# Ids for four blocks in one load, and the last block's single-field chunks moved behind 20 others

## The chip, the cores and the metric

The kernel runs on one core of a Trainium2 chip. The time is device microseconds from the first to the last instruction of one execution; the figure for a kernel is the median of several executions. A core has TensorE (PE in the profile: matrix multiplies and transposes, its weight loads shown as PEld), VectorE (DVE), ScalarE (ACT), GpSimd (POOL), SyncE (SP) and 16 DMA engines. Each of the engines runs its own list of instructions in order and waits for the others through semaphores.

## The reference

A recommender model scores 16384 users. Each user has 69 categorical fields (`batch_user`) and one item (`batch_label`), all of them row numbers of an embedding table of 100001 rows by 96 float32.

```python
u = emb[batch_user]                      # 16384 x 69 x 96
ql = emb[batch_label[:, 0]]              # 16384 x 96
q = broadcast(ql[:, None, :], u.shape)
z = concatenate([q, u, q - u, q * u], axis=-1)
h = dice(z @ W1 + b1, a1)                # 64 wide; dice is a gated activation with a sigmoid
att = (h @ W2 + b2) @ W3 + b3            # one number per user and field
pre = where(batch_user < ITEM_NUM, u * att, 0)
pooled = einsum('gf,bfe->bge', window, pre)      # fields summed into 10 groups
x = concatenate([pooled.reshape(B, G * E), ql], axis=-1)
h = dice(bn(x @ Wf1 + bf1), af1)         # 200 wide
h = dice(bn(h @ Wf2 + bf2), af2)         # 80 wide
return h @ Wf3 + bf3
```

So 16384 x 69 rows of 384 bytes have to be gathered, and each goes through a small network that gives its weight in the sum.

## The kernel before

The users are worked off in 32 blocks of 512. A block's rows come in 69 chunks of 512 rows. The first 64 chunks hold 8 users by 64 fields each; the last five hold one field each (fields 64 to 68) for all 512 users: these are the single-field chunks, "tails" in the code. Two chunks make a pair, and the program is laid out in steps, one pair entering per step: 32 x 69 / 2 = 1104 pairs.

```python
BLK = 512; NBLK = 32; FM = 64; NTAIL = 5; NMAIN = 64; NCH = 69      # NS = 8 users per main chunk
NCOL = NCH * 4 + 4                       # id columns of a block: 4 per chunk, 4 for the items
POOL_LAG = 8; CLOSE = 8
ipool = tile_pool(name="ipool", bufs=2)  # ids
upool = tile_pool(name="upool", bufs=14) # gathered rows of a pair
xpool = tile_pool(name="xpool", bufs=1)  # pre, x1, g1, x2
...
def load_ids(n):                                                    # L136
    t = ipool.tile([P, NCOL], I32, tag="ids", name=f"ids{n}")
    nc.sync.dma_start(out=t, in_=idx[n])                            # L138
    return t
ids = {0: load_ids(0)}
...
def chunk(c):                                                       # L256
    n, k = divmod(c, NCH)
    if n == NBLK - 1:
        k = (k - NTAIL) % NCH            # the last block begins with its tails
    return n, k
```

The main steps of a pair. A gather is one indirect DMA of 128 rows that GpSimd issues, eight per pair. TensorE turns the rows to put the 96 features on partitions; VectorE multiplies by the item's row; four matmul groups give the hidden layer; ScalarE and VectorE do the activation.

```python
def fetch(i, between=None):
    u = upool.tile([P, 8, E], F32, tag="u", name=f"u{i}")
    ...
            for t in range(4):
                gather(rows, u[:, 4 * j + t, :], ids[n][:, 4 * k + t : 4 * k + t + 1])          # issued at L249
                nc.tensor.transpose(ptr[:, t * P : (t + 1) * P], u[:, 4 * j + t, :], ident)     # L305
    ...  # quT = ptr * item row (VectorE, L308 or L315 for a tail), uT = copy of ptr (ScalarE, L317)
def hidden(i, uT, quT):
    ...  # ph = A.uT + Wp.quT (L330, L334; for a tail L327, L332, L334), y = dice(ph) (L336 to L338)
def attend_rows(b, n): ...               # attention numbers of n pairs, L345
def spread(b, n): ...                    # turned, times the group window, L362 and L367
def pool(i):                             # 8 steps after fetch, main chunks only
    ...  # acc = u.T @ rw, 16 small matmuls (L389); VectorE copies the sums to pooled (L398)
def attend_tail(i, j, y, uT):            # tails only, 3 steps after fetch
    ...  # pres[n][:, k - NMAIN, :] = (attention + bb) * uT (L354, L355)
```

A row buffer `u` is free for the next pair when its transposes and its pooling are done; a tail isn't pooled, so its buffer is free after the transposes. When a block's chunks are through, its top network runs in ten steps. The first steps of each half read `pres` (five times), then the item row and the ten `pooled` groups (L428).

```python
        pres[n] = xpool.tile([E, NTAIL, BLK], F32, tag=f"pre{n == NBLK - 1}", name=f"pre{n}")   # L511
...
for n in range(NBLK):                                               # L547
    first, end = n * NCH // 2, ((n + 1) * NCH - 1) // 2
    if n > 0:
        at(first - 20, lambda n=n: ids.__setitem__(n, load_ids(n)))
        at(first - 14, ...head_gather...)                           # item rows, 4 gathers
        at(first - 11, ...head_turn...); at(first - 9, ...head_rows...)
    if n < NBLK - 1:
        for s, work in enumerate(top_steps(n, slice(0, BLK))):
            at(end + POOL_LAG + 4 + s, work)
```

The last block's top network is done in four quarters while its last pairs still run.

Of the kernel before, what the change touches and what calls it, by code (L numbers as in the profile page):

```python
# [32 lines left out]
F32 = mybir.dt.float32  # L33
I32 = mybir.dt.int32
# [4 lines left out]
P = 128  # L39
B, F, E, G = 16384, 69, 96, 10  # L40
# [5 lines left out]
BLK = 512  # L46
NBLK = B // BLK
FM = 64
NTAIL = F - FM
NS = BLK // FM  # L50
NMAIN = BLK // NS
NCH = NMAIN + NTAIL
NQ = BLK // P
NT = NCH * 4
NCOL = NT + NQ
# [4 lines left out]

POOL_LAG = 8

CLOSE = 8


# [45 lines left out]
def rec_kernel(  # L111
    ctx: ExitStack,
    tc: tile.TileContext,
    idx: bass.AP,
    emb: bass.AP,
    rows: bass.AP,
# [4 lines left out]
    nc = tc.nc  # L121

    const = ctx.enter_context(tc.tile_pool(name="const", bufs=1))
    ipool = ctx.enter_context(tc.tile_pool(name="ipool", bufs=2))
# [5 lines left out]
    xpool = ctx.enter_context(tc.tile_pool(name="xpool", bufs=1))  # L130

    def by_field(ap):

        return ap.rearrange("e (s o) -> e s o", o=1).to_broadcast([ap.shape[0], NS, FM])

    def load_ids(n):  # L136
        t = ipool.tile([P, NCOL], I32, tag="ids", name=f"ids{n}")
        nc.sync.dma_start(out=t, in_=idx[n])  # L138
        return t

    ids = {0: load_ids(0)}


    wn = const.tile([P, NEAR.width], F32, name="wn")
# [31 lines left out]
    for i in range(2):  # L176
        t = const.tile([E + 1, BLK], F32, name=f"qT{i}")
# [78 lines left out]
    def chunk(c):  # L256

        n, k = divmod(c, NCH)
        if n == NBLK - 1:
            k = (k - NTAIL) % NCH  # L260
        return n, k

    def head_gather(n):

        q = bpool.tile([P, NQ, E], F32, tag="q", name=f"q{n}")
        for k in range(NQ):
            gather(emb, q[:, k, :], ids[n][:, NT + k : NT + k + 1])
        return q

    def head_turn(n, q):  # L270
        pq = ps_x.tile([E, BLK], F32, tag="x", name=f"pq{n}")
        for k in range(NQ):
            nc.tensor.transpose(pq[:, k * P : (k + 1) * P], q[:, k, :], ident)
        nc.vector.tensor_copy(qTs[n % 2][0:E, 0:BLK], pq)

    def head_rows(n):

        for h in range(2):
            pc = ps_x.tile([P, NMAIN // 8, H1], F32, tag="x", name=f"pc{n}_{h}")
            for k in range(NMAIN // 8):  # L280
                x = (h * NMAIN // 8 + k) * 4 * NS
                nc.tensor.matmul(pc[E:P, k, :], qTs[n % 2][:, x : x + 4 * NS], Cq, start=True, stop=True)  # L282
            nc.scalar.copy(As[n % 2][E:P, h * NMAIN // 8 : (h + 1) * NMAIN // 8, :], pc[E:P])
# [9 lines left out]
    def fetch(i, between=None):  # L293

        u = upool.tile([P, 8, E], F32, tag="u", name=f"u{i}")
        uT = []
        quT = tpool.tile([E, 2, 512], F32, tag="quT", name=f"quT{i}")
        for j in range(2):
            if j == 1 and between:
                between()  # L300
            n, k = chunk(2 * i + j)
            ptr = ps_tr.tile([E, 512], F32, tag="tr", name=f"ptr{i}_{j}")
            for t in range(4):
                gather(rows, u[:, 4 * j + t, :], ids[n][:, 4 * k + t : 4 * k + t + 1])
                nc.tensor.transpose(ptr[:, t * P : (t + 1) * P], u[:, 4 * j + t, :], ident)  # L305
            q = qTs[n % 2][0:E]
            if k < NMAIN:
                nc.vector.tensor_tensor(  # L308
                    quT[:, j, :].rearrange("e (s f) -> e s f", f=FM),
                    ptr.rearrange("e (s f) -> e s f", f=FM),  # L310
                    by_field(q[:, k * NS : (k + 1) * NS]),
                    ALU.mult,
                )
            else:
                nc.vector.tensor_tensor(quT[:, j, :], ptr, q[:, 0:BLK], ALU.mult)  # L315
            uT.append(room(k))
            nc.scalar.copy(uT[j][0:E], ptr)  # L317
        return u, uT, quT
# [98 lines left out]
    def top1(n, cols, h, part, p1):  # L417

        if part == 0:
            p1 = ps_m.tile([DH, BLK], F32, tag="m", name=f"p1_{n}_{h}_{cols.start}")[:, cols]  # L420
        for k in range(part * KTOP // 4, (part + 1) * KTOP // 4):
            if k < NTAIL:
                w, x = V[:, k], pres[n][:, k, cols]
            elif k == NTAIL:
                w, x = wf1[:, G], qTs[n % 2][0:E, cols]
            else:
                w, x = wf1[:, k - NTAIL - 1], pooled[n][:, k - NTAIL - 1, cols]
            nc.tensor.matmul(p1, w[:, h * DH : (h + 1) * DH], x, start=(k == 0), stop=(k == KTOP - 1))  # L428
        if part < 3:
            return p1  # L430
        g1 = xpool.tile([DH, BLK], F32, tag="g1", name=f"g1_{n}_{h}_{cols.start}")[:, cols]
        dice(x1s[n][:, h, cols], g1, p1, bf1c[h], dice1[h])

    def top2(n, cols):
        x2 = xpool.tile([D2, BLK], F32, tag="x2", name=f"x2_{n}_{cols.start}")[:, cols]
        g2 = xpool.tile([DH, BLK], F32, tag="g1", name=f"g2_{n}_{cols.start}")[0:D2, cols]
        p2 = ps_m.tile([D2, BLK], F32, tag="m", name=f"p2_{n}_{cols.start}")[:, cols]
        for i in range(2):
            nc.tensor.matmul(p2, wf2[:, i, :], x1s[n][:, i, cols], start=(i == 0), stop=(i == 1))
        dice(x2, g2, p2, bf2c, dice2)  # L440
        return x2

    def top3(n, cols, x2):
        k0, k1 = cols.start // P, cols.stop // P
        p3 = ps_m.tile([P, k1 - k0], F32, tag="m", name=f"p3_{n}_{cols.start}")
        for k in range(k1 - k0):
            nc.tensor.matmul(p3[:, k : k + 1], x2[:, k * P : (k + 1) * P], wf3, start=True, stop=True)
        nc.vector.tensor_scalar(res[:, n * NQ + k0 : n * NQ + k1], p3, bf3c, None, ALU.add)
# [9 lines left out]
    def top3_last(x2):  # L458

        p3 = ps_m.tile([1, P], F32, tag="m", name="p3_last")  # L460
        nc.tensor.matmul(p3, wf3, x2, start=True, stop=True)
        r = ypool.tile([P, 512], F32, tag="y", name="r1")[0:1, 0:P]
        nc.vector.tensor_scalar(r, p3, bf3c[0:1], None, ALU.add)
        nc.sync.dma_start(out=out[B - P :].rearrange("p o -> o p"), in_=r)

    pooled, pres, x1s, x2s, qs, us, hs, ys, bands, rws, p1s = ({} for _ in range(11))

    def top_steps(n, cols):


        def half(h, part):
            if n not in x1s:
                x1s[n] = xpool.tile([DH, 2, BLK], F32, tag="x1", name=f"x1_{n}")
            p1s[n] = top1(n, cols, h, part, p1s.get(n))

        steps = [lambda h=h, part=part: half(h, part) for h in range(2) for part in range(4)]
        steps.append(lambda: x2s.__setitem__(n, top2(n, cols)))
        if n * BLK + cols.stop < B:
            steps.append(lambda: top3(n, cols, x2s.pop(n)))
        else:  # L480
            steps.append(lambda: top3_last(x2s.pop(n)))
        return steps
# [22 lines left out]
    def fetch_of(k, between=()):  # L505
        def work():
            for j in range(2):
                n = chunk(2 * k + j)[0]
                if n not in pooled:
                    pooled[n] = bpool.tile([E, G, BLK], F32, tag="pooled", name=f"pooled{n}")  # L510
                    pres[n] = xpool.tile([E, NTAIL, BLK], F32, tag=f"pre{n == NBLK - 1}", name=f"pre{n}")  # L511
            u, uT, quT = fetch(k, lambda: [w() for w in between])
            us[k], hs[k] = u, (uT, quT)

        return work
# [4 lines left out]
    def at(step, *work):  # L520
        plan.setdefault(step, []).extend(work)

    close = NPAIR - CLOSE
    for i in range(close):
# [22 lines left out]
    for n in range(NBLK):  # L547
        first, end = n * NCH // 2, ((n + 1) * NCH - 1) // 2
        if n > 0:
            at(first - 20, lambda n=n: ids.__setitem__(n, load_ids(n)))  # L550
            at(first - 14, lambda n=n: qs.__setitem__(n, head_gather(n)))
            at(first - 11, lambda n=n: head_turn(n, qs.pop(n)))
            at(first - 9, lambda n=n: head_rows(n))
        if n < NBLK - 1:
            for s, work in enumerate(top_steps(n, slice(0, BLK))):
                at(end + POOL_LAG + 4 + s, work)
    for f in range(NTAIL):
        at(2 + 2 * f, lambda f=f: tail_weights(f))

# [77 lines left out]
```

## Time and profile before

Three executions took 13199.77 to 13208.66 us, median 13202.15 us. One was recorded by the profiler: a span of 13196.5 us.

| engine | busy us | share of the span | instructions |
|---|---|---|---|
| PE (matmul) | 8794.3 | 67% | 41797 |
| PEld (weight load) | 4570.3 | 35% | 41797 |
| DVE | 3032.1 | 23% | 5324 |
| ACT | 3167.2 | 24% | 4969 |
| POOL | 8455.0 | 64% | 8966 |

The gathers move 440.98 MB over the span, and the DMA engines are busy for some 17% of it. The ids come in 32 loads of 140 KB.

How such a profile is read: a group of instructions is named by its line, engine and operation, with `out<-in`; the busy time of a group stands beside the idle time of the engine before it and what ended that idle time (the releaser). "issue" is idle time without a wait that the profile shows, and "remote" or "another core or an unknown queue" is a release whose source the records don't hold. The chain of waits follows the last instruction back to what let each step start. Starts and ends of matmuls are partly modelled: an instruction that TensorE has taken in need not have finished when its bar ends.

### The profile page before, as it was taken

The numbers are of one execution on the slowest core, as the hardware profiler recorded it, in microseconds if no ns is written. First come the engines' busy times: TensorE is split into PE (matmuls) and PEld (weight loads), VectorE is DVE, ScalarE is ACT, GpSimd is POOL, SyncE is SP. The second block draws the span as 40 slices with busy tenths as digits, with TensorE's granted clock in tenths as the row PEclk, the third lists the DMA queues.
The fourth block names the chain that finished last, engine by engine and source line by source line (L and its number), as shares of the span: only waits on it lengthen the run. The fifth ranks groups of instructions, "written<-read, shape, count | busy, mean of one in ns | idle before, by whom it ended". The sixth has DMA issues, their size and how long they took to land.

```text
span 13196.5 us, 108603 instructions
## 1 busy us (share of the span) xinstructions
PE 8794.3 (67%) x41797; PEld 4570.3 (35%) x41797; DVE 3032.1 (23%) x5324; ACT 3167.2 (24%) x4969; POOL 8455.0 (64%) x8966
## 2 busy tenths in 40 slices
PE   4666666667666676666766667676677666677657
PEld 2333333333333333333333333333333333333334
DVE  2222222222222222222222222222222222222222
ACT  1222222222222222222222222222222222222222
POOL 6666666666666666666666666666666666666664
PEclk6677777777777777777777677777777777777777
DMA  1111111111111111111111111111111111111111
GB/s 38 35 35 34 34 35 34 35 36 34 33 35 34 35 35 34 35 35 35 35 34 35 34 35 34 34 35 35 35 35 35 34 34 34 35 34 35 35 33 22
DMA packets 292259, 454.06 MB, mean 34 GB/s; under 512 B 143906, under 2 KB 148258, under 8 KB 291618
## 3 DMA queue, kind: packets, MB, share of 16 engines
q0 software_dynamic: 286720, 440.98, 16.8%
q8 instruction: 335, 5.49, 0.2%
q1 hardware_dynamic: 4882, 4.90, 0.1%
q14 instruction: 178, 1.46, 0.0%
q10 hardware_dynamic: 144, 1.24, 0.0%
HBM read 446.47 MB, written 0.07 MB: 34 GB/s over the span
## 4 chain that ended last, share of the span: by engine, by line
PE 55%; issue 19%; another core or an unknown queue 16%; POOL 3%; ACT 3%; DVE 3%; DMA 1%; DVEq 0%; POOLq 0%
PE acc L389 11%; PE ptr L305 10%; PE ph L330 9%; PE ph L334 9%; PE p L428 7%; PE prow L345 4%; POOL u L249 3%; PE patt L362 1%; DVE quT L308 1%; PE pa L354 1%; ACT uT L317 1%; ACT y L337 1%; PE ph L327 1%; PE pc L282 1%
## 5 line engine op out<-in xcount | busy, mean ns | idle before, releaser
L249 POOL DMA_INDIRECT u<-in_rows,ids x8832 | 8333.3, 944 | 4574.9 <-issue 2366.2
L389 PE MATMUL acc<-rw,u 128*96 128x20 f32 x16384 | 1934.7, 260 | 1825.7 <-issue 1468.4
L389 PEld LDWEIGHTS acc<-rw,u 128*96 128x96 f32 x16384 | 1921.8, 198 | 2070.5 <-issue 1650.4
L305 PE MATMUL ptr<-ident,u 128*96 128x128 f32 x8832 | 1607.8, 318 | 1428.3 <-issue 1111.7
L305 PEld LDWEIGHTS ptr<-ident,u 128*96 128x96 f32 x8832 | 1087.4, 144 | 2773.9 <-issue 2183.1
L317 ACT COPY uT<-ptr 96x512 f32<-96x512 f32 x2208 | 1283.3, 581 | 3085.5 <-DVE quT L308 1941.0
L336 ACT ACTIVATE y<-ph 128x512 f32<-128x512 f32 x1104 | 659.5, 597 | 5154.5 <-remote 2718.6
L334 PE MATMUL ph<-quT,wn 96*64 96x512 f32 x4416 | 1692.6, 745 | 178.2 <-issue 168.5
L338 DVE TENSOR_TENSOR y<-ph,y 128x512 f32<-128x512 f32 x1104 | 763.5, 692 | 4382.3 <-ACT y L337 2352.5
L330 PE MATMUL ph<-uT,A 128*64 128x512 f32 x4096 | 1633.2, 800 | 140.7 <-issue 136.2
L308 DVE TENSOR_TENSOR quT<-ptr,qT 96x512 f32<-96x512 f32 x2048 | 1336.9, 680 | 1405.4 <-remote 961.0
L398 DVE COPY pooled<-acc 96x160 f32<-96x160 f32 x1009 | 429.9, 426 | 3473.4 <-remote 2069.0
L337 ACT ACTIVATE y<-y,wn,na1c 128x512 f32<-128x512 f32 x1104 | 897.6, 813 | 36.7
L334 PEld LDWEIGHTS ph<-quT,wn 96*64 96x64 f32 x4416 | 446.6, 172 | 1225.4 <-issue 1223.3
L345 PE MATMUL prow<-y,v 128*32 128x512 f32 x2208 | 634.2, 792 | 246.1 <-issue 143.8
L428 PE MATMUL p<-pooled,wf 96*100 96x512 f32 (+1 forms) x1400 | 622.3, 587 | 1.5 <-issue 1.3
L330 PEld LDWEIGHTS ph<-uT,A 128*64 128x64 f32 x4096 | 280.7, 161 | 678.3 <-issue 659.4
L347 ACT COPY row<-prow 128x512 f32<-128x512 f32 (+1 forms) x277 | 161.9, 584 | 1428.4 <-remote 899.3
L362 PE MATMUL patt<-ident,row 128*128 128x128 f32 x1108 | 247.5, 343 | 253.5 <-issue 167.4
L428 PE MATMUL p<-pre,V 96*100 96x512 f32 (+1 forms) x700 | 370.7, 663 | 31.0 <-issue 23.2
L428 PEld LDWEIGHTS p<-pooled,wf 96*100 96x100 f32 x1400 | 236.6, 181 | 297.0 <-issue 296.7
L367 DVE SCALAR_TENSOR_TENSOR rw<-patt,bb,wn 128x320 f32<-128x320 f32 x554 | 273.6, 534 | 146.2 <-remote 84.2
(66 smaller groups left out, 2125.1 us busy)
## 6 DMA issues: line engine op xcount, KB each, us to landing
u<-in_rows,ids POOLq DMA_INDIRECT x8832
ids<-in_idx SPq DMA_DIRECT2D x32, 140.0 KB
q<-in_emb,ids POOLq DMA_INDIRECT x128
wf<-in_far ACTq DMA_DIRECT2D x1, 1209.0 KB
wn<-in_near SPq DMA_DIRECT2D x1, 236.0 KB
out<-r SPq DMA_DIRECT2D x1, 63.5 KB
out<-r SPq DMA_DIRECT2D x1, 0.5 KB
```

The lines of the kernel that those rows point to most:

```text
L249: nc.gpsimd.indirect_dma_start(out=dst, out_offset=None, in_=table, in_offset=bass.IndirectOffsetOnAxis(ap=index, axis=0),)
L305: nc.tensor.transpose(ptr[:, t * P : (t + 1) * P], u[:, 4 * j + t, :], ident)
L308: nc.vector.tensor_tensor(quT[:, j, :].rearrange("e (s f) -> e s f", f=FM), ptr.rearrange("e (s f) -> e s f", f=FM), by_field(q[:, k * NS ...
L317: nc.scalar.copy(uT[j][0:E], ptr)
L330: nc.tensor.matmul(p, As[n % 2][:, k // 4, :], uT[j], start=True, stop=False)
L334: nc.tensor.matmul(p, Wp, quT[:, j, :], start=False, stop=True)
L336: nc.scalar.activation(y, ph, AF.Sigmoid, scale=S_DICE)
L337: nc.scalar.activation(y, y, AF.Identity, bias=a1c, scale=na1c)
L338: nc.vector.tensor_mul(y, ph, y)
L345: nc.tensor.matmul(pr[32 * k : 32 * (k + 1), :], v2, ys[b + k], start=True, stop=True)
L389: nc.tensor.matmul(pa[:, j, 2 * t : 2 * t + 2, :].rearrange("e n g -> e (n g)"), u[:, 4 * j + t, :], rw[:, t, j, :], start=True, stop=True,)
L428: nc.tensor.matmul(p1, w[:, h * DH : (h + 1) * DH], x, start=(k == 0), stop=(k == KTOP - 1))
```

## The change

Three things change. The ids of block 0 are loaded alone, and then those of four blocks at a time, so that 32 loads become 9. In the last block, the single-field chunks no longer come first; 20 main chunks (`EARLY`) come before them. And the last block's `pre` rows no longer have a buffer of their own: all blocks use one, for which block 30's top network is begun earlier and done two steps at a time. The last two save room in SBUF, which the larger id tiles need.

```diff
+NIDS = 4
+EARLY = 20
...
+    ids = {0: const.tile([P, NCOL], I32, name="ids0")}
+    nc.sync.dma_start(out=ids[0], in_=idx0)
+
     def load_ids(n):
-        t = ipool.tile([P, NCOL], I32, tag="ids", name=f"ids{n}")
-        nc.sync.dma_start(out=t, in_=idx[n])
-        return t
-
-    ids = {0: load_ids(0)}
+        t = ipool.tile([P, NIDS, NCOL], I32, tag="ids", name=f"ids{n}")
+        nc.sync.dma_start(out=t.rearrange("p b n -> p (b n)"), in_=idx[(n - 1) // NIDS])
+        for k in range(NIDS):
+            ids[n + k] = t[:, k, :]
...
         n, k = divmod(c, NCH)
-        if n == NBLK - 1:
-            k = (k - NTAIL) % NCH
+        if n == NBLK - 1 and k >= EARLY:
+            k = NMAIN + k - EARLY if k < EARLY + NTAIL else k - NTAIL
         return n, k
...
-                    pres[n] = xpool.tile([E, NTAIL, BLK], F32, tag=f"pre{n == NBLK - 1}", name=f"pre{n}")
+                    pres[n] = xpool.tile([E, NTAIL, BLK], F32, tag="pre", name=f"pre{n}")
...
-            at(first - 20, lambda n=n: ids.__setitem__(n, load_ids(n)))
+            if n % NIDS == 1:
+                at(first - 20, lambda n=n: load_ids(n))
...
-        if n < NBLK - 1:
+        if n < NBLK - 2:
             for s, work in enumerate(top_steps(n, slice(0, BLK))):
                 at(end + POOL_LAG + 4 + s, work)
+        elif n == NBLK - 2:
+            for s, work in enumerate(top_steps(n, slice(0, BLK))):
+                at(end + POOL_LAG + s // 2, work)
...
+    groups = np.concatenate([ids[1:], ids[:1]], axis=0).reshape(-1, NIDS, P, NCOL)
...
-        "idx": ids,
+        "idx0": ids[0],
+        "idx": groups.transpose(0, 2, 1, 3).reshape(-1, P, NIDS * NCOL),
```

(Cut: the new argument `idx0` of the kernel function, and blank lines. The last group of four is blocks 29, 30, 31 and, to fill it up, block 0 again.)

More of the change, by code (lines that the diff above doesn't have):

```diff
@@ L113, in rec_kernel @@
     tc: tile.TileContext,
+    idx0: bass.AP,
     idx: bass.AP,
```

## Prediction

> **What bounds the kernel now.** I read the page first (engines, clock, chain), then the list of waits, then the waits on the id loads, then the place where the change acts, the last block.
>
> The page, parts 1, 2, 4 and 5 (a group's columns: busy us, mean ns of one, idle us before it and its main releaser):
>
> ```profile
> span 13196.5 us, 108603 instructions
> PE 8794.3 (67%) x41797; PEld 4570.3 (35%) x41797; DVE 3032.1 (23%) x5324; ACT 3167.2 (24%) x4969; POOL 8455.0 (64%) x8966
> PEclk6677777777777777777777677777777777777777
> ...
> PE 55%; issue 19%; another core or an unknown queue 16%; POOL 3%; ACT 3%; DVE 3%; DMA 1%; DVEq 0%; POOLq 0%
> ...
> L249 POOL DMA_INDIRECT u<-in_rows,ids x8832 | 8333.3, 944 | 4574.9 <-issue 2366.2
> ```
>
> No engine is full, but two are near their limits in turn. GpSimd issues one gather in 944 ns, and the timeline has 0.30 us between two of them, so 8960 gathers (8832 of `u`, 128 of `q`) need 8960 x 1.249 = 11190 us. TensorE's instructions run at a granted clock of 0.73 on average. The chain of waits is TensorE's own work, and its "unknown queue" parts are stretches in which TensorE completes almost nothing while gathers go on.
>
> The list of waits (us in total, times, longest), GpSimd's rows, and then the row of SyncE's queue:
>
> ```profile
> POOL u L249 <- remote: 967.1, 316, 7.3
> POOL u L249 <- PE acc L389: 557.5, 127, 38.1
> POOL u L249 <- PE ptr L305: 441.7, 227, 5.8
> ```
>
> ```profile
> SPq L138 <- DMA u<-in_rows,ids: 1054.3, 32, 402.4
> ```
>
> GpSimd's waits sum to 967 + 558 + 442 = 1966 us: the 14 row buffers are full and TensorE has to free one. So the span can be written as a sum along GpSimd: 7 us until the first gather, 11190 us of gathers, about 1880 us of pauses, and 122 us from the last gather to the end (13196.5 - 13074). 7 + 11190 + 1880 + 122 = 13199. The change removes no gather and no matmul, so it can only touch the pauses, the start and the end.
>
> The waits on the id loads, line 138 by itself:
>
> ```profile
> L138 SPq DMA_DIRECT2D ids<-in_idx x32: 327/328/1235, 0.7 to 12253.9; - x32
> ...
> who waited for it (us, times):
>   POOL q L249: 5.7, 1
> ```
>
> Of 32 loads only the first was ever waited for, 5.7 us, by the first gather. The change leaves that one as it is.
>
> The last block, in the chain in order of time (start, us, what), GpSimd's timeline, and equal stretches that each begin with a block's first gather (blocks 24 to 31; columns: us, GpSimd busy and gathers, clock, DMA share, GB/s):
>
> ```profile
> 12316.70 28.68 another core or an unknown queue
> 12711.54 42.83 another core or an unknown queue
> 12769.64 19.00 another core or an unknown queue
> ```
>
> ```profile
> 12843.22 0.94 POOL L249 DMA_INDIRECT u<-in_rows,ids  x1 [0.30 <-issue]
> 12865.36 0.94 POOL L249 DMA_INDIRECT u<-in_rows,ids  x1 [21.20 <-PE acc L389]
> ...
> 13073.98 0.94 POOL L249 DMA_INDIRECT u<-in_rows,ids  x1 [0.30 <-issue]
> ```
>
> ```profile
> 9801.00:10001.00 200.00, 132.53 (x141) 0.69 0.18 35
> 10206.00:10406.00 200.00, 125.49 (x133) 0.67 0.17 34
> ...
> 12255.00:12455.00 200.00, 132.49 (x141) 0.72 0.18 35
> 12662.00:12862.00 200.00, 120.83 (x129) 0.69 0.16 32
> ```
>
> See the 42.83 and 19.00 us in which TensorE stood at the join of blocks 30 and 31, and the pause of 21.20 us that GpSimd paid afterwards. The seven stretches before it have 141, 133, 130, 136, 135, 139 and 141 gathers, 136.4 on average; the last one has 129.
>
> **What the Trainium skill says, and whether the trace agrees.** "DMA: Bandwidth & Descriptors", section "Issuing engines are not separate DMA queues": transfers issued by SyncE, ScalarE and GpSimd end on the same 16 engines and interleave. The trace agrees: in the 3 us around the load at 11854 us, 144 packets of the load's queue took 18.1% of 16 engines and 88 gather packets went through as well. That is 0.18 x 3 = 0.54 us of each engine per load, the most by which a load can hold a gather up. The same page, "Anatomy of one DMA", says that a DMA's semaphore wait is done by the issuing sequencer before dispatch. The trace agrees: the 1054.3 us of waiting for a free id tile stand on SyncE's queue, where nothing else is waiting to be done. "TensorE: Matmul & The Clock Gate", section on the HAM clock gate: the clock is half or full, set by recent activity. The mean of 0.733 fits a mix, so shorter stalls would help TensorE a little more than their length; I add nothing for it.
>
> **The change part by part.**
>
> Id loads. 32 loads of 140 KB become one of 140 KB and 8 of 560 KB (the last group holds a block that is not used). The bytes stay about the same (4.5 MB), so engine time shrinks only by fewer descriptors. An upper bound of what the loads cost now is 31 x 0.54 = 17 us, if every one held up the path fully. But TensorE lags GpSimd by several pairs, so a gather that lands 0.5 us late is mostly not felt, and the bytes remain. I take 2 us off.
>
> Start. Both group buffers are free at once, so 2 x 560 KB follow the first ids and the near weights on SyncE's queue, where 140 KB followed before: 980 KB more. In the old start 1.77 MB (ids twice, both weight packs) landed between 2 and 7 us, some 350 GB/s, so this is 980 / 350 = 2.8 us of traffic that now meets the first `q` gathers (6.96 to 11.0 us). The first ids and weights are ahead of it in the queue. I add 1 us.
>
> Order of the last block. Before, the last block's five single-field chunks come first and so join those of block 30: ten chunks, five pairs in a row without pooling. A pair that isn't pooled frees its row buffer after the transposes, not eight steps later, so GpSimd runs further ahead there, TensorE stands for 43 + 19 us, and GpSimd pays with the pause. After, 20 ordinary chunks lie between the two groups of five, and each group looks like every other block end, whose stretches average 136.4 gathers. The shortfall is 136.4 - 129 = 7.4 gathers at 200 / 136.4 = 1.47 us: 11 us. Taken as the time of the first 16 pairs of a block, it is 203 us in the last block against 189 on average: 14 us. I take 13 us off.
>
> The rest of that part. One more copy of pooled sums on VectorE (two half pairs instead of none), 0.43 us, off the path. Block 30's ten top steps come two to a pair from the 8th pair after its end, instead of one to a pair from the 12th: same matmuls, moved.
>
> One buffer for the rows. `pre` of block 31 takes over the tile of block 30. Block 30 is last read in its sixth top step, at step 1069 + 8 + 2 = 1079; block 31 writes it first at step 1079 + 3 = 1082. Three steps at 13202 / 1104 = 11.96 us are some 36 us of slack, so I expect no wait.
>
> Sum: 13202 - 2 + 1 - 13 = 13188 us.
>
> **The rivals.** First, the id loads cause the stalls. For it: about one stall of 20 to 45 us per block in the chain, some 50 to 70 us after a load. If 23 of them went with their loads, at some 28 us each, 640 us would go: 12560 us. Against it: the last load is issued at 12253.9 us, and the stall at 12711.54 us, the longest of the last blocks, comes 458 us later with no load near it. A block's end frees an id tile and brings the single-field pairs in the same stretch, so loads and stalls keep time together without cause. I give it 2%.
>
> Second, the single `pre` buffer makes VectorE wait, and everything in its queue behind it. The slack of 36 us speaks against it, unless TensorE falls into a stall of 40 us just there; then some 10 to 40 us are lost: 13210 to 13230 us.
>
> Third, the stalls are merely dealt out anew. Each step's pause depends on the one before, and blocks take between 397 and 424 us from first gather to first gather. Shifting the start by 1 us and moving SBUF addresses may move the sum of pauses by some 20 us either way. This sets the width of my range. The runs of before lie within 9 us, less than that.
>
> Fourth, the two separated groups cost as much as the joined one: no gain, 13201 us.
>
> **Range and chances.** The middle is 13188 us. The third rival's 20 us, with the gain of the last block between 0 and 25 us, gives 13155 to 13220 us. Two per cent are 264 us, beyond all but the first rival in one direction and beyond anything I can name in the other: faster 2%, within 2% 97%, slower 1%.
>
> **What would show it right or wrong.** Right: 9 id loads, still only the first waited for; 8960 gathers at 944 ns with about 1870 us of pauses; no pause over 20 us in the last block; two shorter stalls there, one near 12700 and one some 120 us later; no wait of VectorE at `pre`. Wrong: the stalls at block ends vanish in three blocks of four (first rival); a long wait of the `pre` multiply on TensorE's top matmul (second); first gather well after 7 us or first transposes late by over 3 us (start).

## The result and the profile after

Six executions of the changed kernel took 13169.13 to 13230.59 us, median 13180.76 us; six of before on the same chip took 13197.66 to 13209.41 us, median 13204.41 us. The ratio is 0.9988, with a 95% interval of 0.9972 to 1.0005, so this pair of sets by itself doesn't exclude that nothing was gained. The profiled execution spans 13170.6 us.

The page of the changed kernel (parts 1, 2, 4 and 5; a group's columns: busy us, mean ns of one, idle us before it and its main releaser):

```profile
span 13170.6 us, 108463 instructions
PE 8747.3 (66%) x41797; PEld 4554.2 (35%) x41797; DVE 3029.0 (23%) x5325; ACT 3167.1 (24%) x4969; POOL 8455.0 (64%) x8966
...
PE 54%; issue 20%; another core or an unknown queue 16%; POOL 4%; ACT 3%; DVE 3%; DMA 1%; DVEq 0%; POOLq 0%
...
L257 POOL DMA_INDIRECT u<-in_rows,ids x8832 | 8333.2, 944 | 4552.4 <-issue 2367.4
```

The picture is the same: equal matmuls and gathers, the same 944 ns per gather, one copy more on VectorE (5325 for 5324). What changed must lie in the waits. The list of waits of the changed kernel, GpSimd's rows (us in total, times, longest), and then the row of SyncE's queue:

```profile
POOL u L257 <- remote: 978.9, 318, 7.4
POOL u L257 <- PE acc L397: 462.2, 107, 39.8
POOL u L257 <- PE ptr L313: 434.0, 201, 5.7
```

```profile
SPq L147 <- DMA u<-in_rows,ids: 54.1, 7, 10.2
```

SyncE waits 54 us for a free id tile where it waited 1054 us, and nobody gains by it: the loads by four (line 147) have no one waiting for them, and the first one (line 142) has the same 5.7 us as before. Each line by itself:

```profile
L147 SPq DMA_DIRECT2D ids<-in_idx x8: 327/328/648, 1.7 to 10209.0; - x8
its engine sat idle before it (us, times) until:
who waited for it (us, times):
```

```profile
L142 SPq DMA_DIRECT2D ids<-in_idx x1: 404/404/404, 0.7 to 0.7; - x1
...
  POOL q L257: 5.7, 1
```

The chain in order of time (start, us, what), GpSimd's timeline (its longest pause in the last block, the next ones are 8.27 and 7.22 us; then the last gather), and stretches of 200 us from about the starts of blocks 28 to 31 (columns: us, GpSimd busy and gathers, clock, DMA share, GB/s):

```profile
7400.63 43.52 another core or an unknown queue
7812.41 41.51 another core or an unknown queue
...
12695.84 43.51 another core or an unknown queue
12855.92 15.71 another core or an unknown queue
```

```profile
12804.39 0.94 POOL L257 DMA_INDIRECT u<-in_rows,ids  x1 [9.40 <-PE acc L397]
...
13051.49 0.94 POOL L257 DMA_INDIRECT u<-in_rows,ids  x1 [0.30 <-issue]
```

```profile
11427.00:11627.00 200.00, 132.31 (x141) 0.70 0.16 35
11841.00:12041.00 200.00, 129.90 (x138) 0.72 0.16 34
12240.00:12440.00 200.00, 132.92 (x141) 0.70 0.17 35
12647.00:12847.00 200.00, 126.63 (x135) 0.76 0.16 34
```

The stall at the end of block 30 is as long as it was (43.51 us), but what follows it has gone: the second stall stands 160 us later and has 15.71 us instead of 19.00, GpSimd's pause is 9.40 us instead of 21.20, and the first 200 us of the last block hold 135 gathers instead of 129.

Along GpSimd, the 25.9 us between the two profiled executions are these. Block 31's first whole pair began 15.1 us earlier (12647.3 for 12662.4), from there to the last gather it took 7.4 us less (404.2 for 411.6), and from the last gather to the end 3.4 us less (119.1 for 122.5). Only the second is where the order was changed.

### The profile page after: what moved, and what is told of

The parts are those of the page before. It is cut to its first block, busy times and chain, and to the rows that moved or that the text cites. A ratio compares the mean times of both kernels' runs of the same rounds, so it can differ in the third digit from the quotient of the medians.

```text
span 13170.6 us, 108463 instructions
## 1 busy us (share of the span) xinstructions
PE 8747.3 (66%) x41797; PEld 4554.2 (35%) x41797; DVE 3029.0 (23%) x5325; ACT 3167.1 (24%) x4969; POOL 8455.0 (64%) x8966
## 3 DMA queue, kind: packets, MB, share of 16 engines
q14 instruction: 177, 1.45, 0.0%
## 4 chain that ended last, share of the span: by engine, by line
PE 54%; issue 20%; another core or an unknown queue 16%; POOL 4%; ACT 3%; DVE 3%; DMA 1%; DVEq 0%; POOLq 0%
PE acc L397 11%; PE ptr L313 9%; PE ph L338 9%; PE ph L342 8%; PE p L436 7%; PE prow L353 4%; POOL u L257 3%; PE patt L370 1%; DVE quT L316 1%; PE pa L362 1%; ACT uT L325 1%; ACT y L345 1%; PE ph L335 1%; PE pc L290 1%
```

## The experiments

They ran on other chips, each beside before: 13313.67 us for the order alone, the changed kernel again, eight times the id loads and 12 row buffers; 13312.74 us for the joins, held buffers in the changed kernel, spread chunks and the slower GpSimd; 13211.57 us for held buffers in the kernel before and the last version; 13287.90 us for the pair that was run together. So ratios to before on the same chip are compared. They are not quite those of the medians: of the changed kernel's second set the ratio says 11 us below before, the medians 2.6 us. The theory: only the order matters, since a row buffer of a single-field pair comes free eight steps early, GpSimd gathers on without a pause, and TensorE stands meanwhile. Rivals: the id loads; a mere dealing out anew of the pauses from run to run.

**The order alone.** The changed order, one `pre` buffer and the earlier top network, with 32 id loads.

```diff
 # on the kernel before
-        if n == NBLK - 1:
-            k = (k - NTAIL) % NCH
+        if n == NBLK - 1 and k >= EARLY:
+            k = NMAIN + k - EARLY if k < EARLY + NTAIL else k - NTAIL
 # and tag="pre", and block 30's top network from end + POOL_LAG, two steps at a time
```

> The order of the last block, the one pre buffer and the earlier top network of block 30, with the ids still loaded for one block at a time (32 loads). Theory 1 (the join of two groups of single-field chunks cost the time, id loads nothing): about 13190 us, 10 to 15 us below before, no pause of GpSimd over 20 us in the last block, 32 loads of which one is waited for. Theory 2 (fewer id loads gave the time): as before, 13200 to 13208 us. Theory 3 (the pauses are only dealt out anew): anything within 20 us of before, and a spread of the runs as wide as the changed kernel's.

Measured: 13303.60 us, ratio 0.9994 (0.9988 to 1.0001), 8 us below before. The longest pause of GpSimd in the last block, here and then with eight times the id loads (below), which has the old order:

```profile
13079.59 0.94 POOL L251 DMA_INDIRECT u<-in_rows,ids  x1 [11.25 <-PE acc L391]
```

```profile
12959.92 0.94 POOL L250 DMA_INDIRECT u<-in_rows,ids  x1 [21.29 <-PE acc L390]
```

**The changed kernel again.** No edit.

> The changed kernel once more, beside the others on the same chip. All theories: 13170 to 13200 us in most runs. If the pauses are dealt out anew from run to run (theory 3), the spread is again several times that of before, and the median may move by 15 us.

Measured: 13311.05 us (13280.72 to 13333.50), ratio 0.9992 (0.9984 to 1.0000), 11 us below before. Here before spreads as much (13291.95 to 13347.27 us), so the wide spread is no mark of the changed kernel. Order alone and whole change differ by 0.0002, 3 us, well inside both intervals; but both intervals reach 1.000, so these two runs don't show by themselves that the order gains. The mirror of this, loads by four with the old order, wasn't tried.

**Eight times the id loads.**

```diff
-        nc.sync.dma_start(out=t, in_=idx[n])
+        for _ in range(8 if n > 1 else 1):
+            nc.sync.dma_start(out=t, in_=idx[n])
```

> The kernel before with each id load from block 2 on issued eight times over, same bytes to the same tile: 210 more loads of 140 KB. Theory 1: 13195 to 13215 us. Theory 2: if 23 loads fewer gave 24 us, a load costs 1 us and this kernel takes some 210 us more, 13410 us; if a load costs the path all of the 0.54 us that its packets hold each DMA engine, 113 us more, 13317 us. If loads caused the stall at each block end, that stall of 20 to 45 us gets several times longer.

Measured: 13310.84 us, ratio 0.9996 (0.9987 to 1.0004). 210 more loads cost between -17 and +5 us, so one costs at most some 5 / 210 = 0.03 us, and 23 fewer should give less than 1 us. The stalls don't grow either: ScalarE's longest wait before the first activation is 41.0 us, in the profile of before 44.9 us. The second theory falls.

**The suspected cost, sixteen times.**

```diff
-        if n == NBLK - 1:
+        if n % 2 == 1:
             k = (k - NTAIL) % NCH
 # and tag=f"pre{n % 2}"
```

> The kernel before with the single-field chunks first in every odd block, so that 16 block ends (not one) join ten single-field chunks and the other 15 block ends have none; pre in two buffers in turn. Theory 1 (a join of five pairs that free their row buffers early costs 13 us more than two ends of two such pairs): 15 x 13 = 195 us over before, ratio 1.010 to 1.020, with a pause of GpSimd of 20 us or more after each join. Theory 2 (id loads): as before, ratio 1.000. Theory 3 (dealt out anew): within 0.3% of before.

Measured: 13430.96 us, ratio 1.0088 (1.0074 to 1.0101). That is 118 us for 15 more joins, 7.9 us each (6.6 to 9.0 us), where 13 us each had been expected. GpSimd's timeline at the pauses after the last two joins, and blocks 25 to 28, of which the first and third begin with a join (columns as above):

```profile
12271.21 0.94 POOL L249 DMA_INDIRECT u<-in_rows,ids  x1 [26.75 <-PE acc L389]
```

```profile
13102.77 0.94 POOL L249 DMA_INDIRECT u<-in_rows,ids  x1 [21.01 <-PE acc L389]
```

```profile
10402.00:10818.00 416.00, 259.20 (x276) 0.72 0.16 33
10818.00:11236.00 418.00, 269.25 (x286) 0.72 0.17 35
11236.00:11650.00 414.00, 260.40 (x276) 0.73 0.16 33
11650.00:12063.00 413.00, 268.27 (x285) 0.74 0.17 35
```

Each join has its pause: 16 of 15.9 to 26.8 us, one every two blocks, ten of them over 20 us, and every one ends on the pooling matmuls of TensorE, line 389. Before had one over 20 us, after its only join, and others of 9 to 17.7 us after ordinary block ends. The blocks that begin with a join take 1.51 and 1.50 us per gather, the two others 1.46 and 1.45 us. The cost of the order is real and repeats: a dealing out anew within 0.3% would not give an interval of 1.0074 to 1.0101.

**The early release taken away.** A pair of two single-field chunks keeps its rows until the step at which others are pooled.

```diff
         if not todo:
+            hold = ps_acc.tile([E, 2, NS, G], F32, tag="acc", name=f"hold{i}")
+            nc.tensor.matmul(hold[:, 0, 0:2, :]..., u[:, 7, :], rw[:, 3, 1, :], start=True, stop=True)
+            nc.vector.tensor_copy(sink, hold[:, 0, 0, 0:1])
             return
```

> The changed kernel in which a single-field pair keeps its row buffer for eight steps as the others do, by one small matmul of its rows at the step of its pooling (its result is thrown away; 69 or so such matmuls in all, under 0.2 us each). If early release lets GpSimd run on and TensorE stand: the stall of 30 to 43 us at block ends is gone (10 to 15 us per pair there, as elsewhere) and GpSimd's lead stays at 7 or 8 pairs. The time: within 0.5% of the changed kernel, as a block's end cost nothing net. If the stall comes from something else in the single-field pairs (their matmuls, the pre multiply): it stays at 30 to 43 us.

Measured: 13165.03 us, ratio 0.9886 (0.9871 to 0.9901). The list of waits, ScalarE's row for the first activation (us in total, times, longest), of the changed kernel in its second set and then of this one, and three of the longest pieces of this one's chain:

```profile
ACT y L344 <- remote: 2333.6, 282, 43.0
```

```profile
ACT y L345 <- remote: 2270.9, 279, 23.7
```

```profile
4649.92 23.71 another core or an unknown queue
6655.66 20.55 another core or an unknown queue
9436.66 23.22 another core or an unknown queue
```

The stalls of 40 us at block ends have gone; the longest left is 23.71 us. After the start, no pause of GpSimd is over 8 us. So early release makes these stalls, with the loads by four in place. But I had expected no gain: the block ends cost some 0.9992 - 0.9886 = 1.06%, 141 us or 4.4 us per block, though 64 matmuls and copies were added. The two profiles show where: counted in pairs after a block's last pair, GpSimd takes 10.8 us per pair from the 5th to the 8th in the changed kernel and 11.6 us here, but then 12.3 us from the 8th to the 19th and 11.6 us here; in the 13 pairs that end 3 before the block's last, both take 12.0 us. The run ahead gains some 2.4 us and costs some 8 us afterwards.

**The single-field chunks spread in every block,** so that no pair has two of them.

```diff
-        if n == NBLK - 1 and k >= EARLY:
-            k = NMAIN + k - EARLY if k < EARLY + NTAIL else k - NTAIL
-        return n, k
+        return n, ORDER[n == NBLK - 1][k]   # single fields at 36, 44, 52, 60, 68; last block 20, 24, 28, 32, 36
```

> The changed kernel with the five single-field chunks of every block 8 chunks apart (places 36 to 68; in the last block 20 to 36, 4 apart), so that no pair is made of two of them. Early release: no stall over 30 us at block ends, GpSimd's lead at 7 or 8 throughout. VectorE gets 4 to 5 half copies per block more, 32 x 4 x 0.4 = 50 us busy, off the path. Time within 0.5% of the changed kernel. If the single-field chunks themselves are slow, their stalls are dealt over five places and their sum stays.

Measured: 13157.55 us, ratio 0.9883 (0.9868 to 0.9898): the same gain by another way, with no added matmul and 64 more copies of VectorE, two per block (5389 instructions for 5325). Again more than I had expected.

**Fewer row buffers.** `bufs=12` in place of 14 for `u`.

> The changed kernel with 12 row buffers in place of 14, so GpSimd can run two pairs (20 us of gathers) less ahead. If TensorE stands at block ends because GpSimd runs ahead there without a pause: the stalls of 40 us at block ends get shorter by 10 to 20 us and the total stays within 1% (13050 to 13310 us). If the buffers' depth hides waits: 2% or more slower, over 13440 us.

Measured: 13292.39 us, ratio 0.9978 (0.9970 to 0.9986), so 0.14% below the changed kernel. Half of the expectation failed, as ScalarE's row shows:

```profile
ACT y L344 <- remote: 2260.4, 265, 43.0
```

The longest stall stays at 43.0 us. GpSimd's lead, counted as pairs gathered less pairs that ScalarE has copied (`uT`), falls from a median of 6.2 pairs to 4.2, but a block's end still adds its two or three pairs: there it reaches 9 and 7 on average. The small gain fits a shorter end: from the last gather (13187.37 us) to the end of the span (13291.3 us) it is 104 us, with 14 buffers 117 us.

**GpSimd made slower.** A memset of 128 x 256 ahead of every four gathers.

> The changed kernel with a memset of 128 x 256 on GpSimd ahead of every four gathers: 2208 of them, some 0.3 to 0.5 us each with what lies around it, 700 to 1100 us of added work on GpSimd. If the pauses of 1850 us are slack of GpSimd and TensorE sets the pace: the pauses shrink by that much and the time stays within 1%. If GpSimd sets the pace and the pauses are forced on top: 5 to 8% slower. If TensorE goes faster whenever no gather is issued: pauses shrink by more than the memsets add, and the time falls.

Measured: 13329.01 us, ratio 1.0015 (1.0007 to 1.0023), 0.23% or 31 us over the changed kernel's. GpSimd's rows in the lists of waits, first of the changed kernel in its second set, then of this one:

```profile
POOL u L257 <- remote: 867.3, 258, 7.1
POOL u L257 <- PE ptr L313: 588.8, 218, 4.7
POOL u L257 <- PE acc L397: 540.5, 92, 40.2
```

```profile
POOL u L258 <- remote: 772.4, 291, 5.7
...
POOL u L258 <- PE acc L399: 400.4, 83, 21.6
POOL u L258 <- PE ptr L315: 299.1, 133, 4.4
```

2208 memsets of 330 ns are some 730 us of work, part of it in the gaps of 0.30 us that gathers leave anyway. GpSimd's waits in these rows fell from 1997 to 1472 us, all its waits from 2328 to 1680 us, and only 31 us came out at the end. So GpSimd's pauses are slack: the time has to pass for TensorE's sake. This doesn't show that TensorE would keep its pace whatever GpSimd does. The memsets too are time without a gather, and the last section shows that TensorE gets most done in such time; fewer or faster gathers weren't tried.

**The kernel before with held buffers,** to see whether anything else in the change gains. The same edit as above, with the old order and 32 loads.

> The kernel before (id loads one block at a time, the two groups of single-field chunks joined, two pre buffers) with the row buffers of single-field pairs held for eight steps. If early release is the whole of what the order of the last block changed: as the changed kernel with held buffers (0.9886 of before), ratio 0.9875 to 0.9900, no pause over 20 us at the join. If the order's gain has another source (the earlier top network, the single pre buffer, the id loads): 8 us or more slower than that, ratio 0.9892 or more.

Measured: 13026.02 us, ratio 0.9866 (0.9844 to 0.9887), below both ranges. After the start no pause of GpSimd is over 8 us, and the stalls have gone with 32 loads too:

```profile
ACT y L337 <- remote: 2476.5, 296, 23.4
```

Another chip than the one of the changed kernel with held buffers, and the intervals overlap; so both ran once more, together.

> The kernel before with held buffers, once more, now beside the changed kernel with held buffers on one chip. If early release is all that the change touched: the two within 8 us of each other (0.06%). If the change has another source of gain, that one is 8 to 25 us slower here.

> The changed kernel with held buffers, beside the kernel before with held buffers on one chip. If early release is all that the change touched: within 8 us of it. If fewer id loads, the earlier top network or the single pre buffer gain too: 8 to 25 us faster.

Measured: before with held buffers 13117.10 us (13113.39 to 13119.94), changed with held buffers 13122.38 us (13120.36 to 13124.98); ratios 0.9870 and 0.9874. The changed kernel is not faster but 5 us slower. With the early release gone, nothing of the change's gain is left.

**A version that beats both.** Spread chunks and 10 row buffers.

> The kernel with the single-field chunks spread in every block, with 10 row buffers in place of 14. As TensorE sets the pace and GpSimd only waits for buffers, a lead of 3 to 4 pairs in place of 7 to 8 should cost nothing in the blocks and shorten the stretch after the last gather (117 us with 14 buffers, 104 us with 12) to 90 us: ratio 0.985 to 0.988. If the lead hides the landing of gathers: new waits of TensorE on gathers and 1% or more slower than with 14, ratio over 0.998.

Measured: 13001.19 us, ratio 0.9846 (0.9828 to 0.9865), the best of all. Its span and its last gather:

```profile
span 12993.1 us, 108558 instructions
```

```profile
12918.08 0.95 POOL L265 DMA_INDIRECT u<-in_rows,ids  x1 [0.30 <-issue]
```

75 us from the last gather to the end, where 90 us were expected. Spread chunks with 14 buffers had 121 us there and a ratio of 0.9883 on another chip; the 0.0037 between the two ratios are 49 us and the shorter end 46 us, so no loss in the blocks is seen. Nor do the transposes wait longer for gathers, 54.5 us in all for 72.2 us. The lead, counted as above, is two pairs (median 2.0), fewer than expected, and it is enough.

## Why the prediction was right

Right in the whole: 13188 us predicted, 13180.76 us measured, within 2% as expected. That the two lie 7 us apart is luck: the steps sum to 14 us off, the medians of that chip say 24 us and the second set of the same two kernels 3 to 11 us. By its steps:

- **The sum along GpSimd.** Gathers at 944 ns and 0.30 us, pauses, start and end are still the whole of the time, and the change altered only pauses. But a sum along an engine doesn't say who sets the pace: slowing GpSimd showed that its pauses are slack.
- **Id loads, 2 us off.** Mis-sized, though by little: 210 added loads cost no more than 5 us, so 23 removed should give under 1 us. The bound of 0.54 us per load was far from reached.
- **Start, 1 us on.** The first gather went from 6.96 to 7.04 us and the fourth transpose of the items from 13.48 to 13.54 us: 0.06 us. The 980 KB more cost next to nothing.
- **Order of the last block, 13 us off.** The mechanism held, the size was too large: 7.9 us per join (6.6 to 9.0) where it was made 15 times more, 7.4 us in the profile of the changed kernel, 8 us for the order alone. I had sized it from one block against the average of the others, whose own scatter is some 4 us, and up to the end of the pause, where the deficit is largest. The stretches didn't begin with a block's first gather either: block 31 has its first at 12657.4 us, half a pair before 12662. Counted from each block's own first gather, the others have 136.6 gathers in 200 us and block 31 has 132, which would have been 7 us; and the blocks' lengths, given as 397 to 424 us, are 401 to 418 us.
- **One buffer for the rows, no wait.** Right. Block 31's five `pre` multiplies waited 3.38 us at most, and for nothing that the profile names; no row of the waits shows them behind the top network's matmuls.
- **The first rival** (id loads make the stalls, 2%) fell three times: with 8 loads the stalls at block ends stay (43.52, 41.51, 43.51 us); with 242 loads the time stays; with 32 loads and held buffers they go.
- **The third rival** (dealt out anew) is what is left of the 25.9 us: the 15.1 us that blocks 0 to 30 gained in one profiled execution have no cause in the code that an experiment could show, and six executions of that kernel lie 61 us apart.
- **The fourth rival** (two groups cost as much as one) isn't excluded by the order alone, but by the 16 joins.
- **Expected signs.** Two stalls in the last block's stretch, some 160 us apart rather than 120, and no pause over 20 us there: seen. "Shorter" held for the second alone; the one of block 30 is as long as ever.

What stayed unseen in the prediction was larger than what it was about. It took every other block's end as the measure of no loss, and so missed that each such end costs some 4 us too: 1.1 to 1.2% in all, which either of two small edits gets back.

## What to carry to other kernels

When a producer runs ahead of a slower engine, look at where its buffers come free: a few tiles that are released earlier than the rest gave it an uninterrupted run here, and the slow engine stood through it. Even release, by holding the odd tiles as long as the others or by mixing them among them, was worth some ten times more here than fewer loads or a better order at the end. And size a suspected cost by making it many times over: one join was 8 us in a spread of 60 us, sixteen were clear.

## What the runs showed of the hardware that was not expected

The longer gathers follow each other without a pause, the less TensorE completes. In the profile of before, its semaphores show 279 stretches of over 8 us without a completed group, 3466 us together. 78% of them end while GpSimd pauses, though it pauses for only 14% of the time, and the median end is 2.9 us after the last gather's issue has ended (the middle half between 2.7 and 3.0 us). The trace holds only 9655 of some 12200 updates of this semaphore, but VectorE and ScalarE, whose records are whole and which wait for TensorE's results, say the same: together they start 0.78 instructions per us on average, 0.32 once gathers have followed each other for over 10 us, and 1.3 in the third and fourth us of a pause of over 1 us.

The bars of the matmuls don't show it. At a block's end, the last bars of a hidden group stand at 6200 to 6201 us, and the activation that waits for the group starts at 6244 us, when the semaphore rises:

```profile
6199.97 1.03 PE L334 MATMUL ph<-quT,wn 96*64 96x512 f32 x4
```

```profile
6244.14 0.60 ACT L336 ACTIVATE y<-ph 128x512 f32<-128x512 f32 x1 [43.54 <-remote]
```

Why is open. The Trainium skill's page "SBUF — State Buffer", section "Who interferes with whom", says that DMA and compute engines don't contend in SBUF, and no run here tells whether the gathers' writes, their semaphores or something in TensorE's own queue is at work. That early release lengthens these stretches, and even release shortens them, is shown (the longest of the changed kernel's second set has 43.8 us, with held buffers or spread chunks 22.4 us); what stops TensorE in them is not. Ten buffers instead of 14 costing nothing that was seen was the other surprise: the lead of six pairs that this kernel pays for in SBUF hid no wait.
